# First slot of a graph-network kernel: loads of x in quarters, sums interleaved one strip sooner

## Chip, core and metric

The kernel runs on one core of a Trainium2 chip. The metric is device time in microseconds (us) of one execution. Three runs of the kernel before gave 1302.4, 1303.8 and 1304.43 us, median 1303.8.

## The reference, cut to what matters

There are 16 graphs (B = 16) with N = 1024 nodes and D = 256 features; `adj` holds zeros and ones, is symmetric and has ones on the diagonal. Two layers follow each other:

```python
# layer 0
e0 = leaky(einsum('bid,bjd->bij', h * a0[:, 0], h))      # leaky: slope 0.2
alpha = sigmoid(where(adj == 1, e0, -max))               # values 2, 3, 4 of adj have their own a1, a2, a3
x = layernorm(x + einsum('bij,bjd->bid', alpha, h) + bias)
# layer 1
Hh = x @ W
s, d = Hh @ a[:256], Hh @ a[256:]
e = where(adj != 0, exp(-leaky_relu(s[:, :, None] + d[:, None, :])), 0)
x = layernorm(x + elu((e @ Hh) / rowsum(e)))
```

The kernel has a fast pass for the case that `adj` holds only zeros and ones, and a general pass behind a flag that the fast pass computes. With these inputs only the fast pass runs, and only it is changed.

## The kernel before

All arithmetic is in 32-bit floats. A graph's 1024 rows are eight tiles of 128. The scores of layer 0 are symmetric, so only the upper triangle is multiplied: **strip** jt is the block of rows of tile jt from its diagonal to the right, made by TensorE from `xT` (x transposed) and `xa` (x transposed and scaled by a0). ACT takes two tanh of each strip into `tb` and `low`, and DVE takes their maximum (line 218): sigmoid of the leaky score is a half of one plus that. `finish` (line 220) adds one, multiplies by the adjacency and writes the strip into `al`; GpSimd then adds two on the diagonal block, which brings in the residual x. The lower triangle is the transposed strip. In graph 0 TensorE transposes it (`mirror`, line 257) and DVE masks it out of PSUM. In all later graphs DVE transposes blocks of 32, SP writes them to a buffer in HBM (`dump`, line 236) and reads them back (`gather`), and DVE masks them (`mask`).

`sum0(b, t)` (line 308) is the sum of layer 0 for tile t: eight matmuls over jt with `al[:, jt, tile t]` as weights and x as the moving operand, then DVE's bias and statistics. After tile 3 and tile 7, GpSimd makes the reciprocal deviations (`center`), ACT scales the tiles (`scale0`), SP saves half of x1 to HBM (`save_x1`) and reads it back in blocks (`fetch_x1`), and DVE turns these (`turn_x1`, line 352) into `x1T`, from which `project` (line 354) makes layer 1's H with the extended weights `Wx`. Two columns of `Wx` hold W times the halves of a; `make_Wx` (line 160) computes them once on DVE through the buffer `tmp`. `check_adj` (line 117) lets ACT test a quarter of the adjacency, and its discarded output also goes to `tmp`, which has one buffer.

The program runs in slots. Slot 0 has layer 0 of graph 0 alone; slot b has the strips of graph b beside the projection of graph b - 1, then the eight sums of layer 0 of graph b, then those of layer 1 of graph b - 1. There is no scheduler: each engine has its instructions in the order in which the Python text issues them (`manual_schedule`), and waits in that order. PSUM has three buffers for strips (`ps_e`), two for mirrors (`ps_t`) and three for sums (`ps_acc`). The loads of the adjacency are issued by GpSimd, everything else by SP, whose DMAs are therefore issued in the text's order too.

Slot 0 (lines 463 to 494) loads x in two halves behind the column `acol` of a0, transposes it by TensorE in four groups of four tiles (`transpose_x`, line 182), and makes strips 0 to 3 with the left half of their `finish` and their mirrors. Then come `make_Wx` and the loads of the next x, once as rows (`load_x(1)`) and once in blocks for xT (`load_blocks`, line 107), into a buffer that held `a` until `make_Wx` has read it. Then it goes over the eight sums, with the strips and mirrors 4 to 7 between sums 0 to 3, and the right half of `finish` of strip t behind sum t.

Of the kernel before, what the change touches and what calls it, by code (L numbers as in the profile page):

```python
# [9 lines left out]
F32 = mybir.dt.float32  # L10
# [4 lines left out]
ALU = mybir.AluOpType  # L15
AX = mybir.AxisListType
PSUM = bass.MemoryType.PSUM

P = 128
HALF = 512  # L20
# [5 lines left out]
CHECKS = 4  # L26
# [3 lines left out]
def one_kind_pass(  # L30
# [31 lines left out]
    nc = tc.nc  # L62
    B, N, D = x.shape
    NT = N // P
    ND = D // P
    HT = HALF // P
# [5 lines left out]
    one = ctx.enter_context(tc.tile_pool(name="one", bufs=1))  # L72
    two = ctx.enter_context(tc.tile_pool(name="two", bufs=2))
    dram = ctx.enter_context(tc.tile_pool(name="dram", bufs=2, space=bass.MemoryType.DRAM))
    small = ctx.enter_context(tc.tile_pool(name="small", bufs=3))
    ps_e = ctx.enter_context(tc.tile_pool(name="ps_e", bufs=3, space=PSUM))
# [5 lines left out]

    xs, adjs = {}, {}

    def load_x(b, pieces=1):
        xs[b] = two.tile([P, NT, D], F32, tag="x", name=f"x_{b}")
        rows = x[b].rearrange("(t p) d -> p t d", p=P)
        n = NT // pieces
        for g in range(pieces):
            nc.sync.dma_start(xs[b][:, ts(g, n), :], rows[:, ts(g, n), :])  # L90

    def load_adj(b, g, columns=None):
# [14 lines left out]
    def load_blocks(dst, src, n0, n):  # L107


        v = src[ds(n0, n), :].rearrange("(nb nn) (c q dd) -> q c nn nb dd", nn=SQ, c=ND, dd=SQ)  # L110
        for c in range(ND):
            for q in range(P // SQ):
                nc.sync.dma_start(
                    dst[ts(q, SQ), c, ds(n0, n)].rearrange("p (nb dd) -> p nb dd", dd=SQ), v[q, c]
                )

    def check_adj(b, n):
        junk = one.tile([P, NT // CHECKS, N], BF16, tag="tmp", name=f"junk_{b}_{n}")
        n_t = NT // CHECKS
        ((_, rows),) = adj_rows(b, n * n_t, (n + 1) * n_t, slice(None))  # L120
        nc.scalar.activation(  # L121
            junk,
            rows,
            AF.Square,
            bias=minus1,
            scale=2.0,
            accum_out=chk[:, b * CHECKS + n : b * CHECKS + n + 1],
        )


    acol = const.tile([P, ND], F32, tag="acol", name="acol")
    with nc.allow_non_contiguous_dma(reason="a column of 256"):
        nc.sync.dma_start(acol, a0.rearrange("(c p) o -> p (c o)", p=P))
    load_x(0, 2)
    ident = const.tile([P, P], F32, tag="ident", name="ident")
    make_identity(nc, ident)
    ident2 = const.tile([P, P], F32, tag="ident2", name="ident2")
# [19 lines left out]
    Wx = const.tile([P, ND, D + 2], F32, tag="Wx", name="Wx")  # L157
    nc.sync.dma_start(Wx[:, :, 2:], W.rearrange("(c p) o -> p c o", p=P))

    def make_Wx():  # L160

        for c in range(ND):
            wprod = one.tile([P, 2, D], F32, tag="tmp", name=f"wprod_{c}")
            for s in range(2):
                nc.vector.tensor_tensor(wprod[:, s, :], Wx[:, c, 2:], a_bc[:, ts(s, D)], ALU.mult)
            nc.vector.tensor_reduce(Wx[:, c, 0:2], wprod, AX.X, ALU.add)


    xTs, xas, als, tbs, mirs = {}, {}, {}, {}, {}
# [1 line left out]
    def new_xT(b):  # L171

        xTs[b] = one.tile([P, ND, N], F32, tag="xT" if b != 1 else "y", name=f"xT_{b}")

    def turn_x(b, c):

        if c == 0:
            xas[b] = one.tile([P, ND, N], F32, tag="xa", name=f"xa_{b}")
        nc.vector.transpose(xTs[b][:, c, :], xTs[b][:, c, :])
        nc.scalar.mul(xas[b][:, c, :], xTs[b][:, c, :], acol[:, c : c + 1])  # L180

    def transpose_x(b, g, c):
        if g == 0 and c == 0:
            new_xT(b)
            xas[b] = one.tile([P, ND, N], F32, tag="xa", name=f"xa_{b}")
        pool, tag = (ps_t, "t") if g == 0 else (ps_e, "e")
        pt = pool.tile([P, HT, P], F32, tag=tag, name=f"pxT_{b}_{g}_{c}")
        for t in range(HT):
            nc.tensor.transpose(pt[:, t, :], xs[b][:, g * HT + t, ts(c, P)], ident)
        flat = pt.rearrange("p t q -> p (t q)")  # L190
        nc.vector.tensor_copy(xTs[b][:, c, ts(g, HALF)], flat)
        nc.scalar.mul(xas[b][:, c, ts(g, HALF)], flat, acol[:, c : c + 1])

    def strip(b, jt):


        if jt == 0:
            als[b] = one.tile([P, NT, N], F32, tag="al", name=f"al_{b}")
        width = N - jt * P
        tb = four.tile([P, N], F32, tag="tb", name=f"tb_{b}_{jt}")  # L200
        tbs[b, jt] = tb
        n_chunks = -(-width // HALF)
        per = -(-(width // P) // n_chunks) * P
        for n, o in enumerate(range(0, width, per)):
            w = min(per, width - o)
            pe = ps_e.tile([P, HALF], F32, tag="e", name=f"pe_{b}_{jt}_{n}")
            for c in range(ND):
                nc.tensor.matmul(  # L208
                    pe[:, 0:w],
                    lhsT=xTs[b][:, c, ts(jt, P)],  # L210
                    rhs=xas[b][:, c, ds(jt * P + o, w)],
                    start=(c == 0),
                    stop=(c == ND - 1),
                )
            low = two.tile([P, HALF], F32, tag="low", name=f"low_{b}_{jt}_{n}")
            nc.scalar.activation(tb[:, ds(o, w)], pe[:, 0:w], AF.Tanh, scale=0.5)  # L216
            nc.scalar.activation(low[:, 0:w], pe[:, 0:w], AF.Tanh, scale=0.5 * SLOPE)  # L217
            nc.vector.tensor_tensor(tb[:, ds(o, w)], tb[:, ds(o, w)], low[:, 0:w], ALU.max)  # L218

    def finish(b, jt, c0=0, c1=N):  # L220


        c0 = max(c0, jt * P)
        nc.vector.scalar_tensor_tensor(  # L224
            als[b][:, jt, c0:c1],
            tbs[b, jt][:, c0 - jt * P : c1 - jt * P],
            1.0,
            adjs[b, jt // HT][:, jt % HT, c0:c1],
            ALU.add,
            ALU.mult,  # L230
        )
# [25 lines left out]
    def mirror(b, t):  # L257

        for j0 in range(t + 1, NT, HT):
            n = min(HT, NT - j0)  # L260
            pt = ps_t.tile([P, HT, P], F32, tag="t", name=f"pal_{b}_{t}_{j0}")
            for q in range(n):
                nc.tensor.transpose(pt[:, q, :], tbs[b, t][:, ts(j0 + q - t, P)], ident)
            for js, rows in adj_rows(b, j0, j0 + n, ts(t, P)):
                nc.vector.scalar_tensor_tensor(
                    als[b][:, js, ts(t, P)],
                    pt[:, js.start - j0 : js.stop - j0, :],
                    1.0,
                    rows,
                    ALU.add,  # L270
                    ALU.mult,
                )
# [32 lines left out]

    x1s, mv0s, r0s = {}, {}, {}

    def sum0(b, t):
        if t == 0:
            x1s[b] = two.tile([P, NT, D], F32, tag="x1", name=f"x1_{b}")  # L310
            mv0s[b] = small.tile([P, NT, 2], F32, tag="mv0", name=f"mv0_{b}")
            r0s[b] = []
        acc = ps_acc.tile([P, D], F32, tag="acc", name=f"acc0_{b}_{t}")
        for jt in range(NT):
            nc.tensor.matmul(  # L315
                acc,
                lhsT=als[b][:, jt, ts(t, P)],
                rhs=xs[b][:, jt, :],
                start=(jt == 0),
                stop=(jt == NT - 1),  # L320
            )
        y = x1s[b][:, t, :]
        nc.vector.scalar_tensor_tensor(y, acc, 0.5, bias_bc, ALU.mult, ALU.add)  # L323
        stats(y, mv0s[b][:, t, :], f"0_{b}_{t}")
        if t % HT == HT - 1:
            g = t // HT
            r0s[b] += center(mv0s[b][:, ts(g, HT), :], f"0_{b}_{g}")

    def scale0(b, t):
        scale(x1s[b][:, t, :], *r0s[b][t])  # L330
# [129 lines left out]

    for g in range(2):
        for c in range(ND):
            transpose_x(0, g, c)
    strip(0, 0)
    for jt in range(HT):
        if jt < HT - 1:
            strip(0, jt + 1)
        finish(0, jt, 0, HALF)  # L470
        mirror(0, jt)
    make_Wx()
    load_x(1)
    new_xT(1)
    load_blocks(xTs[1], x[1], 0, N)
    for t in range(NT):
        sum0(0, t)
        if t < HT:
            finish(0, t, HALF, N)
            strip(0, t + HT)  # L480
        if 1 <= t <= HT:
            finish(0, t + HT - 1)
            if t < HT:
                mirror(0, t + HT - 1)
        if t in (4, 5):
            scale0(0, 2 * t - 8)
            scale0(0, 2 * t - 7)
        if t == 5:
            save_x1(0, 0)
            fetch_x1(0, 0)  # L490
        if t in (5, 6):
            turn_x(1, t - 5)
        if t < CHECKS:
            check_adj(0, t)

    for b in range(1, B):
        prev, done = b - 1, b - 2
# [114 lines left out]
    for t in range(NT):  # L612
        if t < n_first:
            acc = first[t]
# [422 lines left out]
```

## Time and profile before

| | |
|---|---|
| median of three runs | 1303.8 us |
| profiled execution, own time | 1304.77 us |
| its span in the profile | 1303.0 us |
| TensorE busy (PE) | 1265.0 us, 97% of the span |
| DVE busy | 925.4 us, 71% |
| ACT busy | 650.7 us, 50% |
| GpSimd busy (POOL) | 295.3 us, 23% |
| strips of slot 1 start | 57.47 us |
| first long run of sums in slot 1 starts | 92.19 us |

The span is the time from the first to the last instruction of the profiled execution; its own time is 1.8 us longer. Times in all views are microseconds from the start of the span. PE is the matmul side of TensorE, PEld its weight loads; SPq is a DMA issue on SP. "L315" is line 315 of the kernel. A name like `acc<-x,al` says what an instruction writes and reads. In a timeline the bracket at the end of a line is how long the engine was idle before it and what ended that. The chain of waits goes back from the last instruction to whatever released each step; "issue" in it is time for which it shows no releaser.

### The profile page before, as it was taken

The numbers are of one execution on the slowest core, as the hardware profiler recorded it, in microseconds if no ns is written. First come the engines' busy times: TensorE is split into PE (matmuls) and PEld (weight loads), VectorE is DVE, ScalarE is ACT, GpSimd is POOL, SyncE is SP. The second block draws the span as 40 slices with busy tenths as digits, with TensorE's granted clock in tenths as the row PEclk, the third lists the DMA queues.
The fourth block names the chain that finished last, engine by engine and source line by source line (L and its number), as shares of the span: only waits on it lengthen the run. The fifth ranks groups of instructions, "written<-read, shape, count | busy, mean of one in ns | idle before, by whom it ended". The sixth has DMA issues, their size and how long they took to land.

```text
span 1303.0 us, 17447 instructions
## 1 busy us (share of the span) xinstructions
PE 1265.0 (97%) x5445; PEld 1022.0 (78%) x5445; DVE 925.4 (71%) x2000; ACT 650.7 (50%) x1459; POOL 295.3 (23%) x606
## 2 busy tenths in 40 slices
PE   7979999999999999999999999999999999999995
PEld 5758788787877878788787887878778787887884
DVE  5665876868868586786868868587785868768664
ACT  4543544645545564545645545564545735446424
POOL 2212121321212222121221212223121221213203
PEclk9989999999999999999999999999999999999998
DMA  9386487694857948487594956948578594876211
GB/s 215 65 180 118 86 189 140 128 202 84 187 112 170 181 95 193 88 188 155 116 203 82 192 120 155 185 95 198 89 175 172 107 194 83 190 139 129 82 17 68
DMA packets 609173, 181.30 MB, mean 139 GB/s; under 512 B 486200, under 2 KB 591664, under 8 KB 609072
## 3 DMA queue, kind: packets, MB, share of 16 engines
q1 hardware_dynamic: 588480, 138.61, 49.0%
q0 software_dynamic: 20592, 41.48, 18.0%
q8 instruction: 46, 0.75, 0.2%
q14 instruction: 55, 0.45, 0.1%
HBM read 152.44 MB, written 61.14 MB: 164 GB/s over the span
## 4 chain that ended last, share of the span: by engine, by line
PE 82%; issue 5%; SPq 4%; DVE 4%; DMA 3%; POOL 1%; ACT 1%; POOLq 0%; DVEq 0%
PE acc L315 34%; PE acc L419 30%; PE pe L208 13%; PE pH L368 4%; SPq L244 3%; DMA mir<-tb 2%; DVE al L224 1%; DVE tb L240 1%; DVE tb L218 1%; ACT tb L216 1%; DVE al L255 1%; POOL r L285 1%; ACT low L217 0%; DMA x<-in_x 0%; SPq L248 0%
## 5 line engine op out<-in xcount | busy, mean ns | idle before, releaser
L315 PE MATMUL acc<-x,al 128*128 128x256 f32 x2048 | 449.3, 380 | 5.3 <-DVE al L255 5.3
L419 PE MATMUL acc<-H,e 128*128 128x257 f32 x2048 | 448.9, 380 | 0.6 <-DVE e L412 0.6
L315 PEld LDWEIGHTS acc<-x,al 128*128 128x128 f32 x2048 | 386.4, 190 | 62.8 <-DVE al L255 10.9
L419 PEld LDWEIGHTS acc<-H,e 128*128 128x128 f32 x2048 | 387.7, 190 | 58.4 <-DVE e L412 1.3
L208 PE MATMUL pe<-xa,xT 128*128 128x384 f32 (+3 forms) x768 | 267.3, 486 | 0.0
L208 PEld LDWEIGHTS pe<-xa,xT 128*128 128x128 f32 x768 | 141.5, 189 | 86.9 <-issue 46.0
L304 ACT ACTIVATE x<-x,mr,r 128x256 f32<-128x256 f32 x128 | 69.2, 592 | 231.6 <-POOL mr L300 199.9
L412 DVE SCALAR_TENSOR_TENSOR e<-p,pq,adj 128x1024 f32<-128x1024 f32 x128 | 159.8, 1270 | 20.8 <-DMA p<-p_row 17.8
L283 POOL TENSOR_SCALAR ve<-mv 128x4 f32<-128x4 f32 (+3 forms) x51 | 17.9, 350 | 676.5 <-DVE mv L277 671.2
L441 ACT ACTIVATE h<-acc,rinv 128x256 f32<-128x256 f32 x127 | 59.7, 470 | 192.7 <-DVE rinv L436 176.5
L216 ACT ACTIVATE tb<-pe 128x512 f32<-128x512 f32 (+1 forms) x192 | 94.3, 491 | 117.2 <-PE pe L208 78.5
L218 DVE TENSOR_TENSOR tb<-tb,low 128x512 f32<-128x512 f32 (+1 forms) x192 | 103.9, 546 | 60.2 <-ACT low L217 48.9
L368 PE MATMUL pH<-Wx,x1T 128*128 128x258 f32 x512 | 129.4, 387 | 8.5 <-issue 8.4
L435 DVE TENSOR_SCALAR rinv<-acc 128x1 f32<-128x1 f32 x128 | 20.1, 157 | 162.2 <-PE acc L419 162.1
L368 PEld LDWEIGHTS pH<-Wx,x1T 128*128 128x128 f32 x512 | 99.1, 194 | 45.5 <-issue 22.9
L121 ACT ACTIVATE junk<-adj,minus 128x2048 bf16<-128x2048 bf16 x64 | 127.3, 1989 | 0.0
L234 POOL TENSOR_TENSOR al<-ident,al 128x128 f32<-128x128 f32 x128 | 68.2, 533 | 241.2 <-DVE al L224 241.0
L224 DVE SCALAR_TENSOR_TENSOR al<-tb,adj 128x512 f32<-128x512 f32 (+7 forms) x132 | 97.5, 738 | 5.0
L323 DVE SCALAR_TENSOR_TENSOR x<-acc,bias_bc 128x256 f32<-128x256 f32 x128 | 54.0, 422 | 61.9 <-PE acc L315 61.9
L217 ACT ACTIVATE low<-pe 128x512 f32<-128x512 f32 (+1 forms) x192 | 93.0, 485 | 0.0
L255 DVE SCALAR_TENSOR_TENSOR al<-al,adj 128x512 f32<-128x512 f32 (+3 forms) x150 | 76.5, 534 | 1.9 <-DMA al<-mir 1.9
L240 DVE STREAM_TRANSPOSE tb<-tb 128x896 f32<-128x896 f32 (+6 forms) x105 | 74.8, 712 | 3.6
(63 smaller groups left out, 903.7 us busy)
## 6 DMA issues: line engine op xcount, KB each, us to landing
adj<-in_adjT POOLq DMA_DIRECT2D x30, 1024.0 KB, 9.2
x_rows<-x SPq DMA_DIRECT2D x32, 512.0 KB, 4.3
x1T<-x_rows SPq DMA_DIRECT2D x256, 64.0 KB, 2.5
x<-in_x SPq DMA_DIRECT2D x15, 1024.0 KB, 5.9
xT<-in_x SPq DMA_DIRECT2D x120, 128.0 KB, 3.4
out<-y SPq DMA_DIRECT2D x30, 512.0 KB, 5.3
p<-p_row POOLq DMA_DIRECT2D x15, 512.0 KB, 4.3
mir<-tb SPq DMA_DIRECT2D x60, 112.0 KB, 2.4
```

What stands on the lines that cost most here:

```text
L121: nc.scalar.activation(junk, rows, AF.Square, bias=minus1, scale=2.0, accum_out=chk[:, b * CHECKS + n : b * CHECKS + n + 1],)
L208: nc.tensor.matmul(pe[:, 0:w], lhsT=xTs[b][:, c, ts(jt, P)], rhs=xas[b][:, c, ds(jt * P + o, w)], start=(c == 0), stop=(c == ND - 1),)
L216: nc.scalar.activation(tb[:, ds(o, w)], pe[:, 0:w], AF.Tanh, scale=0.5)
L217: nc.scalar.activation(low[:, 0:w], pe[:, 0:w], AF.Tanh, scale=0.5 * SLOPE)
L218: nc.vector.tensor_tensor(tb[:, ds(o, w)], tb[:, ds(o, w)], low[:, 0:w], ALU.max)
L224: nc.vector.scalar_tensor_tensor(als[b][:, jt, c0:c1], tbs[b, jt][:, c0 - jt * P : c1 - jt * P], 1.0, adjs[b, jt // HT][:, jt % HT, c0:c1] ...
L240: nc.vector.transpose(tb, tb)
L255: nc.vector.scalar_tensor_tensor(v, v, 1.0, rows, ALU.add, ALU.mult)
L315: nc.tensor.matmul(acc, lhsT=als[b][:, jt, ts(t, P)], rhs=xs[b][:, jt, :], start=(jt == 0), stop=(jt == NT - 1),)
L368: nc.tensor.matmul(pt, lhsT=x1Ts[b][:, c, ts(t, P)], rhs=Wx[:, c, :], start=(c == 0), stop=(c == ND - 1),)
L412: nc.vector.scalar_tensor_tensor(es[b][:, m, :], p_bcs[b], pqs[b][:, m, 1:2], adjs[b, m // HT][:, m % HT, :], ALU.mult, ALU.min)
L419: nc.tensor.matmul(acc, lhsT=es[b][:, m, ts(t, P)], rhs=Hs[b][m], start=(m == 0), stop=(m == NT - 1),)
```

## The change

- x of graph 0 is loaded in four quarters of two tiles instead of two halves, the first two ahead of `acol`. `transpose_x` takes a quarter at a time: two groups of two tiles for each, in buffers of all three PSUM pools.
- Strips 0, 1 and 2 and mirrors 0 and 1 come before the first sum, instead of strips and mirrors 0 to 3. Each later step has one sum, one strip (t + 3), the finish and mirror of strip t + 2, the right half of finish t for t under 4, and only then the end of the sum on DVE. For that `sum0` is split into `multiply0` and `end0`.
- `make_Wx` takes one of its two parts a call, behind sums 0 and 1 instead of before sum 0. The loads in blocks of the next x follow the second part.
- The checks of the adjacency come one step later; in slot 0, `turn_x` of the next x comes one step earlier, so that its first half lies between the first two and the next two of `scale0`.

```diff
+    load_x(0, NT // 2, 0)
+    load_x(0, NT // 2, 1)
     acol = const.tile([P, ND], F32, tag="acol", name="acol")
     with nc.allow_non_contiguous_dma(reason="a column of 256"):
         nc.sync.dma_start(acol, a0.rearrange("(c p) o -> p (c o)", p=P))
-    load_x(0, 2)
+    load_x(0, NT // 2, 2)
+    load_x(0, NT // 2, 3)
...
-    def transpose_x(b, g, c):
-        if g == 0 and c == 0:
+    def transpose_x(b, g):
+
+        if g == 0:
             new_xT(b)
             xas[b] = one.tile([P, ND, N], F32, tag="xa", name=f"xa_{b}")
-        pool, tag = (ps_t, "t") if g == 0 else (ps_e, "e")
-        pt = pool.tile([P, HT, P], F32, tag=tag, name=f"pxT_{b}_{g}_{c}")
-        for t in range(HT):
-            nc.tensor.transpose(pt[:, t, :], xs[b][:, g * HT + t, ts(c, P)], ident)
-        flat = pt.rearrange("p t q -> p (t q)")
-        nc.vector.tensor_copy(xTs[b][:, c, ts(g, HALF)], flat)
-        nc.scalar.mul(xas[b][:, c, ts(g, HALF)], flat, acol[:, c : c + 1])
+        for c in range(ND):
+            pool, tag = ((ps_t, "t"), (ps_acc, "acc"), (ps_acc if c else ps_e, "acc" if c else "e"), (ps_t, "t"))[g]
+            pt = pool.tile([P, 2, P], F32, tag=tag, name=f"pxT_{b}_{g}_{c}")
+            for t in range(2):
+                nc.tensor.transpose(pt[:, t, :], xs[b][:, 2 * g + t, ts(c, P)], ident)
+            flat = pt.rearrange("p t q -> p (t q)")
+            nc.vector.tensor_copy(xTs[b][:, c, ts(g, 2 * P)], flat)
+            nc.scalar.mul(xas[b][:, c, ts(g, 2 * P)], flat, acol[:, c : c + 1])
...
-    for g in range(2):
-        for c in range(ND):
-            transpose_x(0, g, c)
+
+    for g in range(NT // 2):
+        transpose_x(0, g)
     strip(0, 0)
-    for jt in range(HT):
-        if jt < HT - 1:
-            strip(0, jt + 1)
+    strip(0, 1)
+    for jt in range(2):
         finish(0, jt, 0, HALF)
         mirror(0, jt)
-    make_Wx()
+        if jt == 0:
+            strip(0, 2)
     load_x(1)
-    new_xT(1)
-    load_blocks(xTs[1], x[1], 0, N)
     for t in range(NT):
-        sum0(0, t)
+        multiply0(0, t)
+        if t + 3 < NT:
+            strip(0, t + 3)
+        if t < 2:
+            finish(0, t + 2, 0, HALF)
+        elif t + 2 < NT:
+            finish(0, t + 2)
+        if t + 2 < NT - 1:
+            mirror(0, t + 2)
         if t < HT:
             finish(0, t, HALF, N)
-            strip(0, t + HT)
-        if 1 <= t <= HT:
-            finish(0, t + HT - 1)
-            if t < HT:
-                mirror(0, t + HT - 1)
+        end0(0, t)
+        if t < 2:
+            make_Wx(t)
+        if t == 1:
+            new_xT(1)
+            load_blocks(xTs[1], x[1], 0, N)
+        if 1 <= t <= CHECKS:
+            check_adj(0, t - 1)
         if t in (4, 5):
             scale0(0, 2 * t - 8)
             scale0(0, 2 * t - 7)
+            turn_x(1, t - 4)
         if t == 5:
             save_x1(0, 0)
             fetch_x1(0, 0)
-        if t in (5, 6):
-            turn_x(1, t - 5)
-        if t < CHECKS:
-            check_adj(0, t)
```

More of the change, by code (lines that the diff above doesn't have):

```diff
@@ L83, in one_kind_pass, with load_x @@
     xs, adjs = {}, {}
-    def load_x(b, pieces=1):
-        xs[b] = two.tile([P, NT, D], F32, tag="x", name=f"x_{b}")
+    def load_x(b, pieces=1, g=None):
+        if b not in xs:
+            xs[b] = two.tile([P, NT, D], F32, tag="x", name=f"x_{b}")
         rows = x[b].rearrange("(t p) d -> p t d", p=P)
         n = NT // pieces
-        for g in range(pieces):
+        for g in range(pieces) if g is None else [g]:
             nc.sync.dma_start(xs[b][:, ts(g, n), :], rows[:, ts(g, n), :])
@@ L158, in one_kind_pass, with make_Wx @@
     nc.sync.dma_start(Wx[:, :, 2:], W.rearrange("(c p) o -> p c o", p=P))
-    def make_Wx():
-        for c in range(ND):
[L163 to L166, printed above, removed]
+    def make_Wx(c):
+        wprod = one.tile([P, 2, D], F32, tag="tmp", name=f"wprod_{c}")
+        for s in range(2):
+            nc.vector.tensor_tensor(wprod[:, s, :], Wx[:, c, 2:], a_bc[:, ts(s, D)], ALU.mult)
+        nc.vector.tensor_reduce(Wx[:, c, 0:2], wprod, AX.X, ALU.add)
     xTs, xas, als, tbs, mirs = {}, {}, {}, {}, {}
@@ L306, in one_kind_pass, with multiply0 @@
     x1s, mv0s, r0s = {}, {}, {}
+    accs = {}
     def sum0(b, t):
+        multiply0(b, t)
+        end0(b, t)
+    def multiply0(b, t):
         if t == 0:
@@ L312, in sum0 @@
             r0s[b] = []
-        acc = ps_acc.tile([P, D], F32, tag="acc", name=f"acc0_{b}_{t}")
+        acc = accs[t] = ps_acc.tile([P, D], F32, tag="acc", name=f"acc0_{b}_{t}")
         for jt in range(NT):
@@ L321, in sum0, with end0 @@
             )
+    def end0(b, t):
         y = x1s[b][:, t, :]
-        nc.vector.scalar_tensor_tensor(y, acc, 0.5, bias_bc, ALU.mult, ALU.add)
+        nc.vector.scalar_tensor_tensor(y, accs[t], 0.5, bias_bc, ALU.mult, ALU.add)
         stats(y, mv0s[b][:, t, :], f"0_{b}_{t}")
@@ L459, in acc1 @@
         return pool.tile([P, D + 1], F32, tag=tag, name=f"acc1_{b}_{t}")
-    for g in range(2):
-        for c in range(ND):
-            transpose_x(0, g, c)
+    for g in range(NT // 2):
+        transpose_x(0, g)
     strip(0, 0)
-    for jt in range(HT):
-        if jt < HT - 1:
-            strip(0, jt + 1)
+    strip(0, 1)
+    for jt in range(2):
         finish(0, jt, 0, HALF)
         mirror(0, jt)
-    make_Wx()
+        if jt == 0:
+            strip(0, 2)
     load_x(1)
-    new_xT(1)
-    load_blocks(xTs[1], x[1], 0, N)
     for t in range(NT):
-        sum0(0, t)
+        multiply0(0, t)
[7 more added lines that the diff above has]
+            mirror(0, t + 2)
         if t < HT:
             finish(0, t, HALF, N)
-            strip(0, t + HT)
-        if 1 <= t <= HT:
-            finish(0, t + HT - 1)
-            if t < HT:
-                mirror(0, t + HT - 1)
+        end0(0, t)
[6 more added lines that the diff above has]
+            check_adj(0, t - 1)
         if t in (4, 5):
```

## The prediction

> **What bounds the kernel now.** I read the page first, then the chain of waits over the first 64 us and from 57 to 160 us, then the timeline of the same stretches. The page says that TensorE is busy nearly throughout, so only places where it stands idle, or starts late, can be worth anything:
>
> ```profile
> PE 1265.0 (97%) x5445; PEld 1022.0 (78%) x5445; DVE 925.4 (71%) x2000; ACT 650.7 (50%) x1459; POOL 295.3 (23%) x606
> ```
>
> The chain (start, duration, what) shows slot 0, which is all that the change touches:
>
> ```profile
> 1.22 4.31 DMA x<-in_x
> 5.53 0.14 issue
> 5.67 3.48 PE pxT L189 x16
> 9.15 6.44 PE pe L208 x16
> ...
> 23.91 0.14 issue
> 24.05 0.63 PE pal L263 x4
> 24.67 3.46 PE acc L315 x16
> ```
>
> The reader sees TensorE start at 5.67, when half of x has landed, and then one stall in the slot: 1.6 us before 24.05, behind ACT and DVE. Everything else up to 57.47 is TensorE back to back. So slot 0 can give at most the start plus 1.6. The same view of the next slot:
>
> ```profile
> 57.47 6.44 PE pe L208 x16
> ...
> 76.62 8.43 issue
> 85.05 6.55 PE pH L368 x16
> ...
> 92.19 27.69 PE acc L315 x128
> ```
>
> Here, before the first long run of sums, TensorE waits 8.43 us. From 92.19 it is fed continuously. What counts is therefore not when slot 0 ends but when 92.19 comes. The timeline shows what that idle time hangs on:
>
> ```profile
> 49.97 0.39 SPq L341 DMA_DIRECT2D x_rows<-x  x1
> 59.85 1.25 DVE L352 STREAM_TRANSPOSE x1T<-x1T 128x1024 f32<-128x1024 f32 x1 [1.24 <-DMA x1T<-x_rows]
> 62.06 0.69 DVE L218 TENSOR_TENSOR tb<-tb,low 128x512 f32<-128x512 f32 x1 [0.39 <-ACT low L217]
> 65.95 1.31 DVE L218 TENSOR_TENSOR tb<-tb,low 128x512 f32<-128x512 f32 x2 [0.73 <-ACT low L217]
> 71.57 4.31 SPq L113 DMA_DIRECT2D x1T<-x_rows  x8
> 81.91 0.38 ACT L216 ACTIVATE tb<-pe 128x256 f32<-128x256 f32 x1 [5.70 <-DMA mir<-tb]
> ```
>
> Read from below: strip 6 waits for the dump of strip 2 (its buffer), which SP issues at 76.51, behind the second fetch of x1 (71.57), behind the dump of strip 1, whose DVE transposition ends at 69.40. DVE works towards it from 59.85 with two gaps (0.39 and 0.73), and 59.85 is the landing of x1's first half, saved at 49.97. So **the path to 92.19 runs through save_x1(0, 0)**, not through the end of slot 0's sums.
>
> [...] 3.48 / 16 = 0.218 us for a transposition at the start, 0.76 / 7 = 0.109 later, and 6.55 for 16 pH records after the idle time against 0.87 for 4 before. [...] acol, 1 KB, took 2.1.
>
> **The change part by part.** Times are on the old time axis.
>
> *Four loads, acol behind two of them.* Removed ahead of x: one issue (0.49 us). The first piece is 256 KB instead of 512; the packets of x ran at about 375 GB/s once going, so it is 0.69 shorter: 5.53 - 0.49 - 0.69 = 4.35. By acol's 2.1 of fixed cost it would be 0.73 + 2.1 + 0.69 = 3.5. I take the middle, 3.95, for the landing against 5.53. Bounds: 3.5, and 4.9 (little more than the issue). The other pieces are issued by about 3.2 and land about 0.7 apart; TensorE takes 4 x 0.218 = 0.87 for each, so it doesn't wait for them. Two more SP issues put bias, a, W and x_1 1.0 us later: all are needed long after. acol lands about 5, and ACT needs it then. DVE and ACT do eight pieces of 256 instead of four of 512; nearest rows: 0.42 for 128x256 out of PSUM (L323), 0.47 (L378): beside the transpositions, 0.4 per piece against TensorE's 0.44. Strip 0 starts at 7.5: **-1.6**.
>
> *Sum 0 ahead of strip 3.* TensorE's order becomes strips 0 to 2, mirrors 0 and 1, sum 0, strip 3, mirror 2, sum 1 and so on. The old stall goes: **-1.6**. By the chain's durations: 7.5 + 6.44 + 0.76 + 2.58 + 0.66 = 17.9 (sum 0), +3.46 + 2.15 + 0.55 = 24.1 (sum 1), +3.46 + 1.72 + 0.44 = 29.7 (sum 2), +3.46 + 1.29 + 0.33 = 34.8 (sum 3), +3.46 + 0.86 + 0.22 = 39.3 (sum 4). The four adjacency loads (landed 12.4, 16.6, 20.8, 23.3) are in time, the second with some 0.3 of slack or none.
>
> *What is late next.* Sum 4 reads row 3 right of the diagonal, and finish(0, 3, HALF, N) now stands in iteration 3 behind strip 6's maximum, finish 5 and mirror 5 on DVE. DVE is late there for another reason: check_adj(0, 0) writes "tmp", W a's buffer too. It used to come after both parts; now ACT, with strip 5's tanh queued behind it, must wait for the second part. Iteration 1 on DVE: strip 4's tanh is done at 30.4; maximum 0.69, finish 3, mirror 3 and finish 1's right half 0.28 + 0.69 + 0.66, end of sum 1 1.03, W a 0.75 + 0.69, less overlaps: 35.0. ACT's check then runs to 37.1 (2.1), strip 5's tanh to 38.0. DVE: maximum 5, finish 4, mirror 4, finish 2's half, end of sum 2, 3.2 in all: 41.2; maximum 6, finish 5, mirror 5, finish 3's half 1.75: 43.0. Sum 4 has issued three of eight products (39.3 + 1.3 = 40.6) and waits: **+2.3**. Then 45.2, strip 7 and mirror 6 0.6, three sums 10.4: slot 1's strips start at 56.2 instead of 57.47, 1.3 earlier (-1.6 - 1.6 + 2.3, and roundings). W a itself, 2 x 1.4 on DVE, is moved, not removed.
>
> *The save.* End of sum 3 on DVE: 43.0 + 1.0 = 44.0; before, 44.05. GpSimd's statistics took 3.8 to 47.83, so 47.8 again. ACT then is at the last check (to 48.1), two scales (1.04), xa of x_1's first half, which the change puts ahead of the other two scales (1.15), then those (1.04): save_x1 at 51.4 instead of 49.97: **+1.4**. From save to DVE's turn it took 59.85 - 49.97 = 9.9: 61.3.
>
> *x_1 transposed.* Its eight loads wait for W a's second part (35.0 instead of 27.6), and turn_x asks for them at 47.9 instead of 51.7. They took 12.4 from first issue to last landing, at first against the adjacency loads that end at 34; 35.0 + 12.4 = 47.4 even so: hidden.
>
> *Slot 1.* The strips' tanh and second scales come 1.3 earlier, so DVE finds them ready and its gaps, 0.39 + 0.73, close. The dump of strip 1 is ready 1.4 - 1.1 = **+0.3** later, and SP's row and TensorE's start at 92.19 with it. TensorE's 1.3 become idle time there.
>
> *Sum:* 0.3 on the profiled execution's 1303.0 span and 1304.77 own time (1.8 outside the span): 1305.1. That execution stands 1.0 above the median of the three runs, 1303.8; so 1304.1.
>
> **Rivals.**
> Faster: DVE keeps up. If row 3's half and the end of sum 3 come when TensorE would want them, all of 3.2 (1.6 + 1.6) arrives: sums end 3.2 earlier, and if the save moves too, 92.19 becomes 89.0 and the run 1300.7. For it: DVE is busy for only 19.8 of the 33.0 us from 24.5 to 57.47. Against it: the tmp buffer and DVE's order above. It decides where the save is issued before about 48.
> Slower: the save falls further behind. Its place is ACT's row, checks and xa ahead of the scales; the price is 1:1 beyond the 1.1 that DVE's gaps in slot 1 absorb. From a save at about 53.7 on (49.97 + 1.1 + 2.6) the run is slower by over 0.2%; at 54.0, 1306.7. A late first piece (4.9) alone puts it at 52.4.
> It doesn't do what it says: x lands no sooner in quarters. Then +1.6 on everything, 1305.7.
>
> **How the numbers follow.** 0.2%, about what a measurement of this kernel can tell from no change, is 2.6 us: 1301.2 to 1306.4. Forecast with its bounds (3.5 to 4.9 for the landing is -0.5 to +1.0[...]): 1302.6 to 1306.1, chance 0.49. Pieces no sooner: 0.09, also within. The faster rival 0.28, of which 0.02 comes only in part and stays within; the slower 0.14. So 0.26 faster, 0.60 same, 0.14 slower; the range reaches from the faster rival, 1300.7, to 1306.3.
>
> **What would show it.** In the profile after: first transposition near 4.1 and strips near 7.5; no gap before sum 0, near 17.9; a gap of about 2 us within sum 4, near 41, ended by DVE al; ACT's first check after the second W a; x_rows saved near 51.4 and x1T turned near 61.3; strips of slot 1 at about 56, and its long sums at about 92.5. A save before 49, or the long sums before 90, makes the forecast wrong; so does a save after 53.

## The result and the profile after

The changed kernel takes 1311.8 us (median; 1310.7 to 1312.2) against 1303.6 us of the kernel before on the same chip: ratio 1.0062, 95% interval 1.0052 to 1.0072. It is 8.2 us slower; 1304.1 was forecast, in a range that ended at 1306.3. The profiled execution took 1311.04 us with a span of 1309.3, 6.3 more than the span before. The profiled execution of the kernel before stands 1.2 above its median and this one 0.8 below, so the two traces show 6.3 of the 8.2 us.

TensorE does the same instructions and is busy 3.5 us longer, which is already a hint: the work did not grow, and part of it ran at a lower clock (granted 0.50 from 48.97 to 52.38, as a view further down shows). (In all views a matmul leaves two records and a transposition one: a sum of eight matmuls is x16.)

```profile
PE 1268.5 (97%) x5445; PEld 1023.6 (78%) x5445; DVE 925.9 (71%) x2004; ACT 651.2 (50%) x1463; POOL 293.2 (22%) x606
```

The chain of waits of the first 64 us (start, duration, what):

```profile
2.75 7.78 DMA x<-in_x
10.53 0.14 issue
10.66 1.09 PE pxT L194 x4
11.75 8.04 PE pe L213 x16
...
23.79 3.46 PE acc L326 x16
...
48.83 4.11 PE acc L326 x10
52.94 0.44 PE pe L213 x4
53.38 0.11 PE pal L268
53.49 10.36 PE acc L326 x48
```

Before, the strips started at 9.15, behind one load of 4.31 us; now at 11.75, behind one of 7.78, although that load is half as large. The sixteen records of strips 0 and 1 take 8.04 instead of 6.44. Sum 4 comes in two pieces, and its last ten records (five of its eight products) take 4.11 where ten of this kind take 2.2 (3.46 x 10 / 16). The same view of slot 1:

```profile
63.85 6.44 PE pe L213 x16
...
82.84 8.81 issue
91.65 6.25 PE pH L381 x16
...
98.49 27.69 PE acc L326 x128
```

The long sums start at 98.49 instead of 92.19: 6.3 later, which is all of the difference of the spans (1309.3 - 1303.0). Nothing behind that point differs between the two. The timeline shows where the delay comes in, with most groups left out; the bracket is the idle time before a group and what ended it:

```profile
3.93 1.94 PE L194 MATMUL pxT<-ident,x 128*128 128x128 f32 x8 [3.93 <-DMA x<-in_x]
...
8.29 1.11 PE L194 MATMUL pxT<-ident,x 128*128 128x128 f32 x4 [2.42 <-DMA x<-in_x]
...
10.66 1.09 PE L194 MATMUL pxT<-ident,x 128*128 128x128 f32 x4 [1.26 <-DMA x<-in_x]
...
40.77 2.00 ACT L122 ACTIVATE junk<-adj,minus 128x2048 bf16<-128x2048 bf16 x1 [4.54 <-DVE Wx L169]
...
48.83 4.11 PE L326 MATMUL acc<-x,al 128*128 128x256 f32 x10 [2.17 <-DVE al L229]
...
59.16 0.39 SPq L354 DMA_DIRECT2D x_rows<-x  x1
...
68.16 1.25 DVE L365 STREAM_TRANSPOSE x1T<-x1T 128x1024 f32<-128x1024 f32 x1 [3.17 <-DMA x1T<-x_rows]
```

The first two quarters of x are in early, as forecast (3.93). The third and the fourth are late, and TensorE waits for each. The stall of sum 4 and ACT's wait for `make_Wx` are where the prediction put them, only later. The save comes at 59.16 instead of 49.97.

Why the quarters are late is seen in the table of DMA queues over the first 7 us (queue, kind: packets, MB, share of the 16 engines). q1 is SP's queue with x, q0 GpSimd's with the adjacency. Before:

```profile
q1 hardware_dynamic: 1430, 1.15, 61.9%
q0 software_dynamic: 3, 0.00, 0.3%
```

After:

```profile
q1 hardware_dynamic: 1103, 0.81, 43.8%
q0 software_dynamic: 244, 0.25, 24.2%
```

GpSimd issues its first adjacency load at 1.90 in both. Before, all but 3 packets of the adjacency waited until x was in, at 7.0. After, 244 of its packets move in that time. In the packet records x runs at 185 packets of 1 KB per half microsecond while alone, and at about 55, beside some 60 of the adjacency, from 5.5 on.

### The profile page after: what moved, and what is told of

Its sections match the earlier page's. It is cut to its first block, busy times and chain, and to the rows that moved or that the text cites. A ratio compares the mean times of both kernels' runs of the same rounds, so it can differ in the third digit from the quotient of the medians.

```text
span 1309.3 us, 17454 instructions
## 1 busy us (share of the span) xinstructions
PE 1268.5 (97%) x5445; PEld 1023.6 (78%) x5445; DVE 925.9 (71%) x2004; ACT 651.2 (50%) x1463; POOL 293.2 (22%) x606
## 4 chain that ended last, share of the span: by engine, by line
PE 81%; issue 5%; DVE 4%; SPq 4%; DMA 3%; POOL 1%; ACT 1%; POOLq 0%; DVEq 0%
PE acc L326 33%; PE acc L432 30%; PE pe L213 14%; PE pH L381 5%; SPq L249 3%; DMA mir<-tb 2%; DVE al L229 1%; DVE tb L223 1%; DVE tb L245 1%; DMA x<-in_x 1%; DVE al L260 1%; ACT tb L221 1%; POOL r L290 1%; ACT low L222 0%; SPq L253 0%
## 5 line engine op out<-in xcount | busy, mean ns | idle before, releaser
L425 DVE SCALAR_TENSOR_TENSOR e<-p,pq,adj 128x1024 f32<-128x1024 f32 x128 | 159.8, 1270 | 18.8 <-DMA p<-p_row 15.6
```

The lines of the kernel that those rows point to most:

```text
L425: nc.vector.scalar_tensor_tensor(es[b][:, m, :], p_bcs[b], pqs[b][:, m, 1:2], adjs[b, m // HT][:, m % HT, :], ALU.mult, ALU.min)
```

## The experiments

All times are medians; the interval is that of the ratio to the kernel before (1303.6 to 1304.0 on these chips). "Long sums" is their start in slot 1, 92.19 in the kernel before. Landings and packets come from the trace's DMA records.

**Where acol stands among the quarters.** The first idea was a gap: in both kernels x's packets thin out for 1 to 1.5 us behind the 256 four-byte packets of `acol` (19 to 48 per half microsecond where x alone makes 185), and the change had put these between the quarters. Two kernels move acol, one ahead of all four quarters (shown), one behind them.

```diff
-    load_x(0, NT // 2, 0)
-    load_x(0, NT // 2, 1)
     acol = ...
     nc.sync.dma_start(acol, ...)
+    load_x(0, NT // 2, 0)
+    load_x(0, NT // 2, 1)
     load_x(0, NT // 2, 2)
```

> The changed kernel with the one small load (acol) ahead of all four quarters of x, as in the kernel before; nothing else. Theory (gap): between the second and third quarter acol's 256 small packets empty x's row in the DMA engines, the adjacency's packets get in, and from then on x shares the engines to its end (third quarter landed 8.2, fourth 10.5). With acol first, x runs unbroken: fourth quarter by about 7, strips of slot 0 at 8.5 to 9, and the run at 1304 to 1307 (what the loop alone costs). Rival (pieces): four small loads can't keep the row full; the fourth quarter lands after 9 again and the run stays at 1310 to 1312. Rival (loop): the order of the loop is what costs 8 us; strips at 9, and still 1310 or more.

> The changed kernel with acol behind all four quarters. Theory (gap): first quarter lands at 3.9 as in the changed kernel, fourth by about 6.5; but ACT needs acol for every piece of xa and gets it only at about 7, so that strips start at about 8.9; 1304 to 1307. Rival (pieces): fourth quarter after 9, run 1310 to 1312.

Measured: 1312.13 (1.0048 to 1.0083) and 1313.21 (1.0054 to 1.0088). The idea was wrong. With acol ahead of everything TensorE still waits for the last two quarters:

```profile
9.32 1.12 PE L194 MATMUL pxT<-ident,x 128*128 128x128 f32 x4 [2.93 <-DMA x<-in_x]
11.60 1.08 PE L194 MATMUL pxT<-ident,x 128*128 128x128 f32 x4 [1.16 <-DMA x<-in_x]
```

**The two halves of the change by themselves.** One kernel has the new loop over the sums behind the front of before (two loads, acol first, four transpositions at a time), the other the new front ahead of the old loop.

> The new loop behind the old front (x in two halves behind acol, transposed in groups of four). Theory (gap): the front costs most of the 8 us; here strips start at 9.15 as before, sum 0 at 19.6, the gap within sum 4 is about 2 us, x_rows is saved at about 53 and the run is 1305 to 1307.5. Rival (loop): save at 57 or later and 1310 or more.

> The new front (four quarters, acol between the second and third) ahead of the old loop. Theory (gap): strips start at 11.5 and the first of them run at half clock, 2.4 + 1.6 = 4 later than before; the old loop carries that 1:1: 1306.5 to 1308.5. Rival (loop): within 1 of the kernel before, 1303 to 1304.5.

Measured: loop only 1305.55 (1.0008 to 1.0027), front only 1308.66 (1.0026 to 1.0054). So the front is the larger part, +4.7 against +1.6; together they cost 8.2, more than the sum of the two. The timeline of the loop-only kernel tests the prediction's steps with the front taken out:

```profile
44.44 2.43 PE L321 MATMUL acc<-x,al 128*128 128x256 f32 x10 [2.17 <-DVE al L224]
...
53.12 0.39 SPq L349 DMA_DIRECT2D x_rows<-x  x1
...
62.32 1.25 DVE L360 STREAM_TRANSPOSE x1T<-x1T 128x1024 f32<-128x1024 f32 x1 [3.39 <-DMA x1T<-x_rows]
```

The prediction's 51.4 and 61.3, with its 1.6 for the front put back, are 53.0 and 62.9; measured are 53.12 and 62.32. Its long sums, forecast in the same way at 94.1, came at 92.40: the way from the save to them was shorter than forecast.

**Loads or transpositions.** The changed kernel with x in two loads, acol first, and all else as changed:

```diff
-    load_x(0, NT // 2, 0)
-    load_x(0, NT // 2, 1)
     acol = ...
     nc.sync.dma_start(acol, ...)
-    load_x(0, NT // 2, 2)
-    load_x(0, NT // 2, 3)
+    load_x(0, 2)
```

> The changed kernel with x's slot 0 in two loads again (the weight column first, as before); the transpositions stay in quarters, and the loop stays new. Theory L (four loads are what costs: behind them the adjacency gets to the DMA engines at 4.2 in place of 6.9 and shares them with x): x lands at about 5.5 and 7.0, strips start at 8.7 to 9.2, and the time is that of the new loop with the old front, 1304.5 to 1307. Theory T (transposing in quarters, with two tiles in each PSUM buffer, is what costs): strips start past 10.5 and the time stays at 1309 to 1313.

Measured: 1306.37 (1.0013 to 1.0028), strips from 8.95. Transposing in quarters costs little (0.8 against the loop alone); four loads are what costs (5.4 of the 8.2).

**The adjacency kept back.** In the changed kernel GpSimd reads a column of x's second quarter before it issues the adjacency:

```diff
+    held = const.tile([P, 1], F32, tag="held", name="held")
+    nc.gpsimd.tensor_copy(held, xs[0][:, 3, 0:1])
     for h in range(2):
         for g in range(2):
             load_adj(0, g, ts(h, HALF))
```

> The changed kernel, four loads of x as in it, with the adjacency's loads issued on GpSimd only when the second quarter of x has landed (GpSimd reads one column of it first). Theory L (sharing with the adjacency): x's third and fourth quarter land by 6.0 and 7.0 instead of 8.2 and 10.5, strips start at 7.8 to 8.6 instead of 11.5, the adjacency's first load still lands by about 11, and the time falls to 1303 to 1306.5. Rival S (small loads are slow by themselves, or each waits for the one ahead): the third quarter still lands at 8 or later, strips at 11 or later, and the time is 1310 to 1314.

Measured: quarters landed at 3.6, 4.3, 6.4 and 7.0, strips from 8.19 instead of 11.54 on the timeline; 1307.81 (1.0025 to 1.0041). So the adjacency's packets are what held the quarters up. The time fell by 4.0 and not by the 5 to 9 expected: strips 0 and 1 took 8.19 (6.61 in the same view of the kernel before), with weight loads 0.86 us apart up to 10.76 and 0.43 apart from 11.49, so that the clock rose only between those two, and the stall of sum 4 cost as much as in the changed kernel (4.11 for the ten records behind it). One number was far off: the adjacency's first load landed at 15.6 and not at 11. Issued at 4.50, it came behind W (4.24) and beside x_1 (4.73).

**What lets the adjacency in.** Theory O: over both queues loads go through in the order in which they are issued. Rival N: it is the number or size of x's loads. The first test puts the bias between x's halves in the kernel before, so that the second half is issued at 2.27, behind the adjacency's 1.90:

> The kernel before with one thing changed: SP issues the bias between x's two halves, so that the second half is issued at about 2.3 instead of 1.7, after GpSimd's first adjacency load (1.90). Theory O (loads go through in the order of their issue over both queues, and what SP issues after 1.90 shares the engines with the adjacency): the first half still lands by 5.5, the adjacency's packets begin by about 5.5 instead of 6.9, the second half lands at 8.5 to 11 instead of 7.0, strips start at 10 to 13 instead of 8.8 to 9.2, and the time rises by 1.5 to 4, to 1305.5 to 1308. Rival N (it is the number or the size of the loads that lets the adjacency in): the second half lands by 7.6 and the time stays within 1 us of before.

Measured: 1307.06 (1.0015 to 1.0033), the second half landed at 8.93 instead of 7.01. But the adjacency's packets came later than by 5.5: only 4 had moved by 7.0, and the bias, issued at 1.73, had itself taken until 7.2. The time agrees with O, but a slow bias would have given much of it too. The second test leaves SP's row alone and moves two adjacency loads ahead of the identity on GpSimd, still in the kernel before:

```diff
+    for g in range(2):
+        load_adj(0, g, ts(0, HALF))
     make_identity(nc, ident)
...
-    for h in range(2):
-        for g in range(2):
-            load_adj(0, g, ts(h, HALF))
+    for g in range(2):
+        load_adj(0, g, ts(1, HALF))
```

> The kernel before with the first two adjacency loads issued on GpSimd ahead of the identity, at about 0.75 instead of 1.90, so ahead of x's two halves (1.22 and 1.73). Theory O (loads go through in the order of issue over both queues): the adjacency's packets begin before 4.5 instead of 6.9, and x's halves, two large loads as before, land at 7 or later and 9 or later instead of 5.5 and 7.0; strips start at 10.5 or later and the time rises by 1.5 or more. Theory N (large loads keep the adjacency out, whatever the order): the halves land by 6.0 and 7.5 and the time stays within 1 us of before.

Measured: 1305.91 (1.0011 to 1.0025). GpSimd could issue only at 1.25, not 0.75, which by luck fell between x's halves (1.22 and 1.73). The timeline:

```profile
1.25 1.77 POOL L98 DMA_DIRECT2D adj<-in_adjT  x2 [0.82 <-POOLq L1026]
...
5.38 1.94 PE L190 MATMUL pxT<-ident,x 128*128 128x128 f32 x8 [5.38 <-DMA x<-in_x]
...
8.60 1.97 PE L190 MATMUL pxT<-ident,x 128*128 128x128 f32 x8 [1.28 <-DMA x<-in_x]
```

The half issued 0.03 us ahead of the adjacency landed at 5.24, as ever; the half issued 0.48 behind it landed at 8.56 instead of 7.01, and 167 packets of the adjacency moved in the first 7 us instead of 3. Size and number of x's loads are as before, so N falls as the cause of the sharing. Nor is it a fixed delay of GpSimd's queue: from the issue of the adjacency to its first packet it took 4.9 us in the kernel before and 2.3 in the changed kernel. From the other side, the changed kernel with acol first and GpSimd reading acol (landed 2.84) instead of x, which puts the adjacency's issue at 3.03, behind all four quarters:

> The changed kernel, four loads of x, with the weight column first and GpSimd reading that column before it issues the adjacency, so that the adjacency is issued at about 3.0, behind all four quarters, and waits for none of them. Theory O: the adjacency's packets begin at about 6, the quarters land by 4.1, 4.8, 5.6 and 6.5, strips start at 7.4 to 8.2, and the time falls from 1311.8 to 1305 to 1308 (the stall of sum 4 and its half clock are still in it). Theory N: the third and fourth quarter land at 8 or later and the time is 1309 or more.

```profile
4.35 2.89 PE L196 MATMUL pxT<-ident,x 128*128 128x128 f32 x12 [4.35 <-DMA x<-in_x]
...
7.71 1.09 PE L196 MATMUL pxT<-ident,x 128*128 128x128 f32 x4 [0.48 <-DMA x<-in_x]
```

Here 2 packets of the adjacency moved in the first 7 us; three quarters were transposed in one go, the fourth landed at 7.58. Strips started at 8.59, where 7.4 to 8.2 was expected; why the fourth quarter came 1.5 behind the third isn't shown. The time is 1308.4 (1.0024 to 1.0055, four executions; the profiled one, 1305.67, was the quickest), just above the 1305 to 1308 that was expected. The loads in one table:

| kernel | x's loads issued at | adjacency's first | its packets by 7.0 us | x landed at |
|---|---|---|---|---|
| before | 1.22, 1.73 | 1.90 | 3 | 5.53, 7.01 |
| adjacency ahead | 1.22, 1.73 | 1.25 | 167 | 5.24, 8.56 |
| bias between the halves | 1.22, 2.27 | 1.90 | 4 | 5.25, 8.93 |
| after | 0.73, 1.22, 2.24, 2.75 | 1.90 | 244 | 3.8, 4.5, 8.2, 10.5 |
| acol first | 1.22, 1.73, 2.23, 2.75 | 1.90 | 218 | 4.1, 5.2, 9.3, 11.5 |
| acol last | 0.73, 1.22, 1.73, 2.23 | 1.90 | 161 | 3.5, 4.3, 7.9, 10.1 |
| adjacency behind four | 1.22, 1.73, 2.24, 2.75 | 3.03 | 2 | 4.2, 4.9, 6.1, 7.6 |

The loads of x issued ahead of the adjacency's first landed by 7.6, but for one; those issued behind it landed at 8.2 to 11.5. Two rows fit less well. The third quarter of "acol last", issued 0.17 us ahead, landed only at 7.9. And with the bias between the halves the second half, issued behind, landed at 8.93 although only 4 packets of the adjacency had moved by 7.0.

**The loop: buffer, save, order.** Three kernels change the new loop behind the front of before, one after the other: the junk of `check_adj` gets a buffer of its own; then the four scalings, the save and the fetch come ahead of the check and of xa in the iteration of sum 4; then `finish(0, t, HALF, N)` is issued straight after `multiply0(0, t)`.

```diff
-        junk = one.tile([P, NT // CHECKS, N], BF16, tag="tmp", ...)
+        junk = one.tile([P, NT // CHECKS, N], BF16, tag="junk", ...)
...
+        if t == 4:
+            for k in range(HT):
+                scale0(0, k)
+            save_x1(0, 0)
+            fetch_x1(0, 0)
...
         multiply0(0, t)
+        if t < HT:
+            finish(0, t, HALF, N)
         if t + 3 < NT:
             strip(0, t + 3)
```

> New loop with the front of before, and check_adj's junk in a buffer of its own instead of the one that the products of the W a parts use. Theory tmp: the check no longer waits for the second part on ACT, strip 5's tanh comes some 4 us sooner, the right half of strip 3 is finished before sum 4 needs it, the 2.17 us stall of sum 4 falls under 0.5, the save of x1 goes from 53.1 to about 51, and the time to 1302.5 to 1304.5 (with the shared buffer: 1305.55). Rival D (the order of DVE alone sets the stall): the stall stays at 1.5 or more and the time at 1304.5 to 1306.5.

> As the kernel with the junk's own buffer, and in the iteration of sum 4 the four scalings of x1, its save and its fetch come ahead of the check and of the weighting of slot 1's xT on ACT. Theory: the save goes out at 46 to 49 instead of 53, x1T is turned by 57 to 59 instead of 62.3, so that nothing of slot 1 waits for it, and the time is 1300.5 to 1303, under the kernel before. Rival: slot 1 is bound by its own strips and by DVE; the time is that of the kernel with the junk's own buffer within 1 us.

> The new loop with the front of before, the junk's own buffer, the early save, and the right half of strip t finished straight after the products of sum t are issued, ahead of strip t+3's maximum. Theory: the stall of sum 4 (1.25 us) goes, the last sum ends 1.2 sooner, the save goes out at about 49.3, and the time is 1301 to 1303. Rival: slot 1 is bound elsewhere (its own strips' way through DVE and the queue), and the time stays at 1303 to 1304, that of the kernel with the stall.

Measured: 1304.43 (1.0001 to 1.0019), 1303.42 (0.9989 to 1.0007) and 1301.89 (0.9981 to 0.9998). The own buffer ended ACT's wait but only part of the stall; what is left of it is the order on DVE:

```profile
37.12 2.00 ACT L122 ACTIVATE junk<-adj,minus 128x2048 bf16<-128x2048 bf16 x1
...
43.74 2.42 PE L321 MATMUL acc<-x,al 128*128 128x256 f32 x10 [1.25 <-DVE al L224]
```

Both theories for that kernel were half right. The early save came at 50.57 where 46 to 49 was expected, since the statistics of sum 3 still ended at 48.4, and the fetch gave most of its gain back (10.6 from save to turn, 9.0 without it). With the order changed too, sum 4 runs through in one piece and the save comes at 49.02:

```profile
40.72 3.62 PE L321 MATMUL acc<-x,al 128*128 128x256 f32 x16
...
49.02 0.39 SPq L349 DMA_DIRECT2D x_rows<-x  x1
...
58.75 1.25 DVE L360 STREAM_TRANSPOSE x1T<-x1T 128x1024 f32<-128x1024 f32 x1 [2.35 <-DMA x1T<-x_rows]
```

Its long sums start at 89.12, 3.1 ahead of the kernel before. This version is faster than both kernels: by 1.7 us than before, with an interval that only just leaves out no change (0.9998), and by 9.9 than after.

**The changed kernel without its stall, and four loads in the best loop.**

> The changed kernel with its own front, with the junk's own buffer and the right half of strip t finished straight after the products of sum t. Theory: sum 4 doesn't stall (2.17 before) and no half-clock stretch of 3.41 us follows it, so that its time falls by 3 to 4.5 from 1311.8, to 1307 to 1309; what is left is the front's 4 us. Rival: the stall is only moved to sum 5 or to the save, and the time stays at 1310 to 1312.

> As the kernel with no stall, but with x in four loads and quarters transposed as they come, the weight column ahead of all four, and the adjacency's loads held until the second quarter has landed. Theory: with neither the adjacency nor the column's lull between the quarters they land about 0.7 apart (4.1, 4.7, 5.4, 6.1), strips start at 7.2 to 8.0 instead of 8.8 to 9.0, and the time is 0.8 to 2 us under the kernel with no stall and under the kernel before, 1299.5 to 1302. Rival: the adjacency, issued 2.5 us later, is now what finish and the mirrors wait for, or the clock rises later; the time is that of the kernel with no stall or above.

> The best loop (no stall at sum 4, early save) with four loads of x, the weight column first, and the adjacency issued behind them at about 3.0. Theory: strips start at 7.4 to 8.2 instead of 8.9, the adjacency's first load lands by 11.5 instead of 13 to 15 as when it waited for the second quarter, nothing waits for it, and the time is 1300.5 to 1302, 0 to 1.4 us under the same loop with two loads (1301.9). Rival: what the quarters gain ahead of the strips (0.8 us) is lost again to the adjacency or ahead of slot 1, and the time is 1302 to 1304.

Measured: 1307.17 (1.0018 to 1.0037), 1303.57 (0.9990 to 1.0007) and 1305.48 (1.0001 to 1.0018). The first has the front of the changed kernel, the junk's own buffer and the new place of finish: 4.6 of the 8.2 us are gone. The 3.6 that stay are of the size of what the front costs alone (4.7). The other two have the best loop with four loads, the adjacency held behind the second quarter or behind acol. Both lose to two loads (1301.89); the first is where its rival had put it, the second above even that. Strips start at 8.09 and 8.71 instead of 8.90, far from the 7.5 of the prediction, as the last quarter lands at 7.2 and 7.7. In the first the adjacency landed only at 15.9 and TensorE waited 0.84 for DVE ahead of a mirror, and its long sums start at 89.23, level with two loads. In the second strips 0 and 1 took 8.59 (6.61 in the first), and the long sums start at 92.40. Both traces also have one wait in the middle of the run, in slot 8, that no other trace has at more than 0.4 us. In the first of the two:

```profile
679.32 0.47 ACT L457 ACTIVATE y<-acc,rinv 128x256 f32<-128x256 f32 x1 [6.72 <-DMA out<-y]
...
679.85 4.40 PE L434 MATMUL acc<-H,e 128*128 128x257 f32 x19 [1.71 <-ACT y L457]
```

ACT waits for a store of the output, in the same place for 7.03 in the second and for 2.67 with two loads. It makes all behind it 2.0 and 1.8 us later, so in its trace the first loses to two loads in slot 8 and not ahead of the long sums. Why the store is late, and whether other executions have it too, isn't settled.

## Why the prediction was wrong

**The step that failed** is in the first part: "The other pieces are issued by about 3.2 and land about 0.7 apart; TensorE takes 4 x 0.218 = 0.87 for each, so it doesn't wait for them." The packets' 375 GB/s were measured while x was alone on the engines, and the prediction carried that rate over to quarters issued 0.3 and 0.9 us behind the adjacency. Measured: quarters at 3.8, 4.5, 8.2 and 10.5, TensorE waiting 2.4 and 1.3 for the last two, strips from 11.75 instead of 7.5. That is 4.2 us. (The third rival, "x lands no sooner in quarters", came nearest, but it too left out the adjacency: the last of x landed at 10.5, 3.5 later than before.) From the moment that both queues have packets the trace shows about 55 of x and some 60 of the adjacency per half microsecond; the page alone doesn't give the order of issue that the table above shows, in which two halves landed at 5.53 and 7.01 while 3 packets of the adjacency moved.

**A second term was missing: the clock.** It rose at 14.84 instead of 8.85 and made strips 0 and 1 1.6 longer. In the traces of the kernel before and of the changed one all changes of the clock lie whole multiples of 3.41 us apart, so they cut a trace into windows of that length. Busy time by engine in the window ahead of the rise in the kernel before, and in the two last windows ahead of it in the changed kernel (columns: stretch, length, PE, PEld, DVE, ACT, GpSimd, granted clock, DMA share, GB/s; ahead of the first change the column of the clock tells nothing). Before:

```profile
5.43:8.85 3.42, 3.19 (x15) 3.22 (x16) 1.74 (x3) 1.17 (x2) 1.35 (x3) 1.00 1.06 215
```

After:

```profile
8.01:11.43 3.42, 1.88 (x8) 1.51 (x9) 0.92 (x3) 0.90 (x2) 0.00 (x0) 1.00 1.14 220
11.43:14.84 3.41, 3.41 (x6) 1.46 (x5) 0.78 (x2) 0.90 (x2) 0.00 (x0) 1.00 1.17 252
```

Behind the window with 1.88 us of TensorE's work the clock did not rise, behind the one with 3.41 it did. Over both whole traces it rose five times, each time behind a window with TensorE busy for 3.19 to 3.42 us, and fell five times, behind windows with 0.00 to 1.24. Behind a window with 2.30 it stayed down and behind one with 1.57 it stayed up; what happens between these figures the two traces don't tell. (The ends of matmuls are modelled in a trace, so the figures are no finer than that.) In the window ahead of the rise at 8.85 TensorE did transpositions alone, 3.19 us of them. So in the changed kernel the gaps of 2.4 and 1.3 between the quarters cost their length, and the late clock came with them. In other runs the late clock shows in the length of strips 0 and 1, 6.61 in the timeline of the kernel before. Two kernels that kept the adjacency away had gaps of 0.77 (adjacency held) and 0.85 (adjacency behind all four, in the best loop) between transpositions, and took 8.19 and 8.59; with gaps of 0.44 (adjacency held, in the best loop), 0.48 (adjacency behind four) and 1.28 (adjacency ahead) it was 6.61, 7.20 and 7.19. The length of the gap alone doesn't give it.

**The stall of sum 4 was right, its price was not.** Forecast 2.3, ended by DVE al; measured 2.17, ended by DVE al. But it set the clock back, as the same view of two later windows of the changed kernel shows:

```profile
45.56:48.97 3.41, 1.24 (x6) 0.51 (x5) 3.34 (x9) 2.57 (x5) 0.45 (x1) 1.00 0.51 80
48.97:52.38 3.41, 3.41 (x9) 2.67 (x10) 0.74 (x3) 0.00 (x0) 2.09 (x6) 0.50 0.00 0
```

One window of 3.41 us had TensorE busy for 1.24, and the next ran at 0.50: the ten records took 4.11 instead of the 2.43 of the loop-only kernel, 1.7 us. The prediction had no such term for sum 4. Seven traces have this stall of 2.17 us. In four (the changed kernel, acol first, acol last, adjacency held) the ten records behind it took 3.78 to 4.11, in three (loop only, two loads with quarter turns, adjacency behind four) 2.42 or 2.43. In the changed kernel the whole stall, 46.66 to 48.83, lay in one window; that the place of the stall among the windows is what sets the four and the three apart is an estimate from this one trace. How many of the executions without a trace paid the 1.7 isn't known.

**The rest of the chain held.** 4.2 + 1.6 + 1.7 = 7.5 put the forecast's 56.2 for slot 1's strips at 63.7; measured 63.85. (The forecast's bracket, -1.6 - 1.6 + 2.3 "and roundings", gives 0.9 and not 1.3 earlier; it is its sum of durations, 56.2, that is used here.) ACT's first check waited for the second W a (4.54 idle). From the save to the turn of x1T the forecast had 9.9, measured are 9.0, and from there to the long sums it had 31.2, measured are 30.3. So the long sums came at 98.49, 6.0 behind the forecast's 92.5, though the save was 7.8 behind its: slot 1 absorbed 2.9 us of a late save (98.49 - 59.16 against 92.19 - 49.97) and not the 1.1 that the forecast allowed.

**The gains.** The 1.6 of the old stall ahead of the sums did come: no gap stands before sum 0. The 1.6 of the earlier start did not, and not even the kernels that clear the adjacency away got more than 0.8 of it. The faster rival ("DVE keeps up") named the right obstacles, the tmp buffer and DVE's order: with both removed, the save moved ahead and x in two loads the long sums begin at 89.12, where it had said 89.0. By the medians that is 1.7 us faster than before, where it had forecast 3.1.

**The slower rival** gave the right sign and a wrong mechanism: it saw the save past 53.7, and the save was indeed at 59.16, but ACT's row had little to do with it; the delay came from x and the clock. Its rule of 1:1 beyond 1.1 would have made 59.16 a loss of 8.1; the long sums lost 6.3, as slot 1 absorbed more.

## What to carry to other kernels

The 375 GB/s read from the trace held while x was alone; beside the adjacency x moved 55 packets per half microsecond instead of 185. Before cutting a load in pieces, look at what the other queues have issued by the time each piece goes out, not at when their packets ran before. The piece that is needed last decides: here the first quarter landed at 3.8, but the adjacency got in ahead of the last, which landed at 10.5, and the strips started at 11.75. The stall of 2.17 us cost its own length and, in the changed kernel's trace, 1.7 more at a clock of 0.50; with gaps of 2.4 and 1.3 between the quarters the clock rose at 14.84 instead of 8.85; and the scratch buffer shared by two engines turned the moved computation into a wait of 4.54 for ACT, the engine that was not moved.

## What the runs showed of the hardware

- In seven kernels that differ in the order of issue, the loads of x issued ahead of the adjacency's first landed by 7.6, but for one at 7.9; those issued behind it landed at 8.2 to 11.5. A half megabyte issued 0.03 us ahead landed at 5.24, although the adjacency was issued 4 us before that; a quarter issued 0.17 ahead landed at 7.9. How this comes about the runs don't tell.
- In the changed kernel x's queue of 1 KB packets fell from 185 to about 55 per half microsecond once the adjacency's ran beside it: the two together moved less than the one alone had (240 GB/s against 375).
- In the changed kernel a stall of 2.17 us lay within one window of 3.41, in which TensorE was busy for 1.24, and the clock granted in the next 3.41 us was 0.50. Of seven traces with such a stall four had 3.78 to 4.11 us for the ten records behind it, and three 2.42 or 2.43.
- In the traces of the kernel before and of the changed one the clock rose five times, behind windows of 3.41 us with TensorE busy for 3.19 to 3.42, and fell five times, behind windows with 0.00 to 1.24. The 3.19 were transpositions alone.
